# A graph kernel's gather units: from one feature group over four blocks in three banks to one block of rows with all 192 features in one bank, with norm factors and residuals on GpSimd

## The chip, the cores and the metric

The kernel runs on one core of a Trainium2 chip. The metric is the device time of one execution in microseconds (us). Before the change it was 928.25 us, the median of three runs (928.08 to 928.56 us).

Engines are named as the profile names them: PE is the matrix engine, PEld its loading of the stationary operand (the "weights"), DVE the vector engine, ACT the scalar engine, POOL GpSimd, SP the engine that issues the DMAs. Matmuls write to PSUM, which is used here in eight banks of 128 x 512 float32.

## The reference, cut to what matters

There are 128 graphs of 128 nodes with 64 features. Two layers follow each other, each with a residual and a layer norm:

```python
# layer 0
mask = adj > 0
h    = relu((x @ W1a)[:, :, None, :] + (x[:, :, None, :] - x[:, None, :, :]) @ W1b + b1)
hm   = einsum('bjkh,bjk->bjh', h, mask)             # 192 hidden features
x    = layernorm(x + hm @ W2 + deg[..., None] * b2)
# layer 1
agg  = einsum('bmn,bnd->bmd', adj, x)
h    = elu(elu(agg @ W1 + b1) @ W2 + b2)            # 128 hidden features
x    = layernorm(x + h @ W3 + b3)
```

Inside `relu` stands `a[j] + c[k]`, with a part that depends on node j alone and a part that depends on its neighbour k alone. Only neighbours count, and a row has few of them: about 6% of the entries of `adj` are positive.

## The kernel before, in words

Two graphs ("a pair") are worked on at a time, 64 pairs in all. In each pair the rows j of a graph are sorted by their number of neighbours. Each row then gets as many slots as its place in the sorted order allows, and slot s of row j holds its s-th neighbour. The table `BANKS` (line 43) gives four blocks of sorted rows with 9, 12, 22 and 15 slots a row: 504, 504, 176 and 330 slots, 1514 in all (the constant `E`). A second, dense path (`dense`, line 772) would take pairs that do not fit; it is not run in the profile.

**Gather units** (lines 704 to 744). A unit works in one of four PSUM banks (`edges`, `NE = 4`), and has three steps:

- *seed*: ACT copies the row part `aj` into the bank, repeated over the slots (L714);
- *gather*: PE adds the neighbour part `cp`, selected by the one-hot matrix `oh`, into the same bank. `cp` is held in three bfloat16 parts that add up to float32, so there are three matmuls, k = 0, 1, 2;
- *reduce*: DVE sums the absolute values over the slots into `sums` (L739).

A unit before is (pair, c, i). The feature group c = 0 or 1 means features 0 to 127 of the first or second graph; its matmuls (L725) use all 128 x 128 cells of the PE array. The group c = 2 holds features 128 to 191 of both graphs: for each k there are two matmuls (L729), each with 64 weight columns, one for the upper and one for the lower half of the partitions. The index i is one of three banks' worth of slots (504, 504, and 176 + 330 = 506). So a pair has 9 units with 3 matmuls (or 3 x 2 half-width ones) of some 504 columns each, and 12 seeds and 12 reduces, one for each block. The next unit on the same bank follows in the same lane (`lane`, line 755).

**The other steps of a pair.** `prepare`, `sort_x`, `project_a`, `sort_mask` and `turn` (lines 413 to 592) prepare a pair three rounds ahead: mask, degrees and ranks (L433 spreads the degrees over the partitions by matmul, L441 compares), the permutation (L450), the sorted x (L463, L465), the projections (L477 to L504), the correction for unused slots (L523 to L538), the slot numbers (L561) and the one-hot matrix `oh` (L572). `finish` (line 636) follows the units: correction (L642), product with W2 (L646 to L653), return to the given order with the residual added by a matmul with the identity (L662, L664), layer norm, layer 1 (L671 to L690), its last product with the residual again by a matmul with the identity (L694, L696), layer norm, and the output DMA (L700).

**The layer norm** (`norm`, line 594): ACT copies y out of PSUM (L597), DVE takes the statistics from PSUM (L603) and forms variance + eps (L605), POOL raises to the power -1/2 (L610), DVE forms the shift (L613), and two ACT activations apply scale and shift (L619).

**What sets the order.** `Flow` (line 278) is a planner that runs when the program is built. Every step is a `yield` with an engine, an estimated cost, the events it needs and the number of PSUM banks it takes out of four (`m0` to `m3`). The planner emits the steps, among those that could start next on an engine, by their due times; `ROUND` (13.0), `PACE` and `STEP` give these. Each engine then works its instructions in the emitted order, and semaphores hold what is not ready.

Of the kernel before, what the change touches and what calls it, by code (L numbers as in the profile page):

```python
# [39 lines left out]
EPS = 1e-5  # L40


BANKS = (((72, 128, 9),), ((30, 72, 12),), ((0, 8, 22), (8, 30, 15)))
# [3 lines left out]
def gnn_kernel(ctx: ExitStack, tc: tile.TileContext, x, adj, w1, b1, w2, b2,  # L47
# [12 lines left out]
    for blocks in BANKS:  # L60
        base, row = E, []
        for p0, p1, s in blocks:
            row.append((p0, p1, s, E - base))
            E += s * (p1 - p0)
        assert E - base <= 512
        LAY.append((base, E - base, row))
# [57 lines left out]
    nc.vector.memset(onesb, 1.0)  # L124
    small = const([P, P], BF16, "small")
    nc.vector.memset(small, 1.0 / P)
    mhalf = const([P, 2], F32, "mhalf")
    nc.vector.memset(mhalf, -0.5)
# [38 lines left out]
    for base, n, row in LAY:  # L167
        for p0, p1, s, off in row:
            nc.gpsimd.iota(slotf[:, base + off:base + off + s * (p1 - p0)],
                           pattern=[[2, s], [0, p1 - p0]], base=1, channel_multiplier=0,  # L170
                           allow_small_or_imprecise_dtypes=True)
    for p0, p1, s in sorted((b for bank in BANKS for b in bank), reverse=True):

        nc.vector.tensor_scalar(steps, jcol[:, 0:1], p1 / P, float(s - prev),
                                op0=OP.is_lt, op1=OP.mult)
        nc.vector.tensor_add(slots, slots, steps)
        prev = s
# [4 lines left out]
    for p0, p1, s in (b for bank in BANKS for b in bank):  # L182
        nc.vector.memset(srow[:, :, p0:p1], float(s))
# [52 lines left out]
    with tc.tile_pool(name="ps_s", bufs=2, space=bass.MemoryType.PSUM) as ps_s:  # L236
# [16 lines left out]
        nc.vector.tensor_sub(c3r, c3r, t[:, H1:H1 + O])  # L253
        nc.vector.tensor_scalar(v1s[F:F + 1], v1s[F:F + 1], 1.0, None, op0=OP.add)
# [95 lines left out]
def sparse(tc, env):  # L350
# [21 lines left out]
    ROUND = 13.0  # L372
    AHEAD = 3
    PACE = ROUND / (3 * NB)
# [23 lines left out]
    def dve(n):  # L398
        return 0.08 + n / 960
# [13 lines left out]
    def prepare(p):  # L413
# [21 lines left out]
        ev, key = yield ("PE", 2 * mm(N) + 0.1, [ev], 1, spread)  # L435
# [8 lines left out]
        ev, = yield ("DVE", 2 * dve(N) + 0.2, [ev], 0, rank)  # L444
        flow.give(key, ev)
        permb = d["permb"] = prep.tile([P, 2, N], BF16, name="permb")

        def permute():
            for s in range(2):
                nc.vector.tensor_scalar(permb[:, s, :], g.iotb, pos[:, s:s + 1], None,  # L450
                                        op0=OP.is_equal)
        ev, = yield ("DVE PORT", 0.36, [ev], 0, permute)
# [45 lines left out]
    def project_a(p, xT, ev):  # L498
# [30 lines left out]
        ev, eb = yield ("PE", 0.38, [have, event("mtp", p)], 1, short)  # L529
# [11 lines left out]
    def sort_mask(p, ev):  # L541
# [25 lines left out]
        for i, (base, n, row) in enumerate(LAY):  # L567
            for p0, p1, sl, off in row:
                w = p1 - p0
                c = slice(base + off, base + off + sl * w)  # L570
                e, = yield ("DVE PORT", 0.07 + sl * w / 860, [ev], 0,
                            lambda: nc.vector.tensor_tensor(  # L572
                                oh[:, :, c].rearrange("p b (s w) -> p b s w", w=w),
                                vp[:, :, p0:p1].rearrange("p b (o w) -> p b o w", o=1)
                                .to_broadcast([P, 2, sl, w]),
                                g.slotc[:, c].rearrange("p (b s w) -> p b s w", b=1, w=w)
                                .to_broadcast([P, 2, sl, w]),
                                op=OP.is_equal))
            happened(e, "oh", p, i)
# [14 lines left out]
    def norm(yps, ev, name):  # L594

        y = work.tile([P, 2, O], F32, name="y", bufs=6)
        evy, = yield ("ACT", act(2 * O), [ev], 0, lambda: nc.scalar.copy(flat(y), yps[:, :2 * O]))  # L597
        st = work.tile([P, 2, 3], F32, name="st", bufs=12)
        ve = work.tile([P, 2], F32, name="ve", bufs=12)

        def stats():

            nc.vector.bn_stats(st.rearrange("p s t -> p (s t)"),  # L603
                               yps[:, :2 * F].rearrange("p (s f) -> p f s", s=2))
            nc.vector.tensor_scalar(ve, st[:, :, 2], 1.0 / F, EPS, op0=OP.mult, op1=OP.add)  # L605
        ev, = yield ("DVE", 0.38, [ev, evy], 0, stats)
        flow.give(yps, ev)
        rs = work.tile([P, 2], F32, name="rs", bufs=12)
        ev, = yield ("POOL PORT", 0.72, [ev], 0,
                     lambda: nc.gpsimd.tensor_tensor(rs, ve, g.mhalf, op=OP.pow))  # L610
        nb = work.tile([P, 2], F32, name="nb", bufs=12)
        ev, = yield ("DVE", 0.1, [ev], 0,
                     lambda: nc.vector.scalar_tensor_tensor(nb, st[:, :, 1], -1.0, rs,  # L613
                                                            op0=OP.mult, op1=OP.mult))
        o = work.tile([P, 2, F], F32, name=name, bufs=6)

        def apply():
            for s in range(2):
                nc.scalar.activation(o[:, s, :], y[:, s, :], AF.Identity, bias=nb[:, s:s + 1],  # L619
                                     scale=rs[:, s:s + 1])  # L620
        ev, = yield ("ACT", 2 * act(F, 2), [ev], 0, apply)
        return o, ev
# [13 lines left out]
    def finish(p):  # L636
# [3 lines left out]
        ev, = yield ("POOL PORT", 1.05, [event("corr", p)] + [event("sums", p, c, i) for c in range(3)  # L640
                                                for i in range(NB)], 0,
# [19 lines left out]
        def unsort(t):  # L661
            nc.tensor.matmul(t[:, :2 * O], ident, flat(xx), start=True, stop=False)  # L662
            for s in range(2):
                nc.tensor.matmul(t[:, s * O:(s + 1) * O], d["permT"][:, s, :],  # L664
                                 ys[:, s * O:(s + 1) * O], start=False, stop=(s == 1))
        ev, t = yield ("PE", 0.6, [ev, event("permT", p)], 1, unsort)
        x1, ev = yield from norm(t, ev, "x1")

# [23 lines left out]
        def last(t):  # L692
            nc.tensor.matmul(t[:, :2 * O], onesb[:, :P], flat(g.c3p), start=True, stop=False)
            nc.tensor.matmul(t[:, :2 * O], ident, flat(x1), start=False, stop=False)  # L694
            for s in range(2):
                nc.tensor.matmul(t[:, s * O:(s + 1) * O], h2[:, s * N:(s + 1) * N], g.v3s,  # L696
                                 start=False, stop=(s == 1))
        ev, t = yield ("PE", 0.83, [ev], 1, last)
        o, ev = yield from norm(t, ev, "o")
# [3 lines left out]

    units = [(p, c, i) for p in range(NP) for c in range(3) for i in range(NB)]

    def unit(u, ev):
        p, c, i = units[u]
        d, e = S[p], edges[u % NE]
        base, n, blocks = LAY[i]

        def seed():
            for p0, p1, sl, off in blocks:
                w = p1 - p0
                nc.scalar.copy(e[:, off:off + sl * w].rearrange("p (s w) -> p s w", w=w),  # L714
                               d["aj"][:, c:c + 1, p0:p1].to_broadcast([P, sl, w]))
        ev, = yield ("ACT", 0.12 * len(blocks) + n / 1200,
                     [ev, event("aj", p), [T0[0] + pace(u)] if T0 else [0.0]], 0, seed)
# [3 lines left out]
        def gather():  # L721
            cp, oh = d["cp"], d["oh"]
            for k in range(3):
                if c < 2:
                    nc.tensor.matmul(e[:, :n], cp[:, k, c, 0:P], oh[:, c, base:base + n],  # L725
                                     start=False, stop=(k == 2), skip_group_check=True)
                else:
                    for s in range(2):
                        nc.tensor.matmul(e[s * HB:(s + 1) * HB, :n], cp[:, k, s, P:H],  # L729
                                         oh[:, s, base:base + n],  # L730
                                         start=False, stop=(k == 2), skip_group_check=True)
        ev, = yield ("PE", 3 * mm(n) + 0.06, [ev, event("cp", p), event("oh", p, i)], 0, gather)

        def reduce():
            if "sums" not in d:
                d["sums"] = work.tile([P, 3, N], F32, name="sums")
            for p0, p1, sl, off in blocks:
                w = p1 - p0
                nc.vector.tensor_reduce(d["sums"][:, c, p0:p1],  # L739
                                        e[:, off:off + sl * w].rearrange("p (s w) -> p w s", w=w),  # L740
                                        AX.X, OP.add, apply_absolute_value=True)
        ev, = yield ("DVE", 0.08 * len(blocks) + n / 960, [ev], 0, reduce)
        happened(ev, "sums", p, c, i)
# [233 lines left out]
```

## Time and profile before

| what | value |
|---|---|
| median of three runs | 928.25 us |
| the profiled execution: its time / its span in the trace | 928.32 us / 925.7 us |
| mean granted PE clock | 0.991 |
| busy share PE, PEld, DVE, ACT, POOL | 94%, 60%, 88%, 77%, 55% |
| matmul records | 6739 |
| the DMA engines' share (the main queue) | 8.1% |

The span is the time from the first to the last instruction of the profiled execution; 2.6 us of its own time lie outside. "Busy" is the union of an engine's instruction records. Those of PE overlap, since a matmul's record includes the time from its last column to its result. So the starts of matmuls tell how fast PE takes them, and the busy share does not. The profile gives, behind PE and PEld rows, the part of the array that an instruction uses as rows\*columns: 128\*128 is the whole array, 128\*64 one half of its columns, 64\*128 one half of its rows.

The first gather matmul starts at 42.2 us and the last one at 902.0 us of the span. What lies ahead is the set-up of constants and the preparation of the first pairs, and behind it the end of the last pair.

### The profile page before, as it was taken

How to read it: one execution, taken by the hardware profiler on the slowest of the kernel's cores; microseconds unless marked ns; L12 is line 12 of the kernel's file. 1: busy time of each engine (PE TensorE's matmuls, PEld its weight loads, DVE VectorE, ACT ScalarE, POOL GpSimd, SP SyncE). 2: the span in 40 equal slices, each digit the busy share in tenths (PEclk: the TensorE clock that was granted, in tenths of full speed). 3: DMA queues.
4: the chain of work that ended last, by engine and by line, in shares of the span. 5: the costliest groups of instructions: out<-in, count | busy, mean ns of one | idle time of the engine just before them, and what ended most of it. 6: DMA issues, size and time to landing. Idle time of an engine off the chain costs nothing. (4 is left out here: it accounts for less than half of the span.)

```text
span 925.7 us, 19643 instructions
## 1 busy us (share of the span) xinstructions
PE 867.1 (94%) x6739; PEld 556.4 (60%) x6740; DVE 813.8 (88%) x2278; ACT 717.3 (77%) x2050; POOL 506.6 (55%) x654
## 2 busy tenths in 40 slices
PE   2689999999999999999999999999999999999994
PEld 1456666665665665666665666666666666666663
DVE  7699889989989989989989989999999999999972
ACT  0577887788788788788788788888878887888772
POOL 1565555665556565556565556565556555555521
PEclk9999999999999999999999999999999999999996
DMA  1100100100110110110100010110011001000000
GB/s 29 43 10 21 25 15 21 24 21 16 24 24 13 24 24 14 24 25 12 25 23 15 22 24 12 25 24 16 21 25 24 16 21 25 16 23 22 7 8 12
DMA packets 63580, 18.84 MB, mean 20 GB/s; under 512 B 46257, under 2 KB 63474, under 8 KB 63474
## 3 DMA queue, kind: packets, MB, share of 16 engines
q1 hardware_dynamic: 63474, 17.52, 8.1%
q8 instruction: 55, 0.90, 0.4%
q14 instruction: 51, 0.42, 0.1%
HBM read 13.24 MB, written 4.19 MB: 19 GB/s over the span
## 5 line engine op out<-in xcount | busy, mean ns | idle before, releaser
L739 DVE TENSOR_REDUCE sums<-e 128x56 f32<-128x504 f32 (+3 forms) x768 | 395.0, 542 | 33.6 <-PE e L725 16.9
L714 ACT COPY e<-aj 128x504 f32<-128x504 f32 (+2 forms) x768 | 366.1, 486 | 74.3 <-DVE sums L739 67.4
L725 PE MATMUL e<-oh,cp 128*128 128x504 bf16 (+1 forms) x1152 | 281.7, 375 | 1.8 <-ACT e L714 1.7
L610 POOL TENSOR_TENSOR rs<-ve,mhalf 128x2 f32<-128x2 f32 x128 | 90.6, 708 | 228.2 <-DVE ve L605 223.9
L725 PEld LDWEIGHTS <-cp 128*128 128x128 bf16 x1152 | 106.1, 97 | 89.5 <-DVE sums L739 1.1
L729 PE MATMUL e<-oh,cp 128*64 128x504 bf16 (+1 forms) x1152 | 157.5, 382 | 1.1 <-ACT e L714 1.1
L572 DVE TENSOR_TENSOR oh<-vp,slotc 128x1008 bf16<-128x1008 bf16 (+2 forms) x256 | 153.9, 601 | 3.2 <-ACT vp L564 3.0
L642 POOL TENSOR_TENSOR hm<-sums,corr 128x384 f32<-128x384 f32 x64 | 73.6, 1151 | 45.8 <-DVE sums L739 42.3
L629 ACT ACTIVATE e<-m,mone 128x256 f32<-128x256 f32 x128 | 62.6, 489 | 32.4 <-PE m L688 30.9
L493 POOL CAST cp<-r 128x512 bf16<-128x512 f32 x64 | 48.9, 765 | 70.5 <-DVE r L490 70.4
L729 PEld LDWEIGHTS <-cp 128*64 128x64 bf16 x1152 | 53.9, 109 | 42.9 <-issue 18.2
L495 POOL TENSOR_TENSOR cp<-r,cp 128x512 bf16<-128x512 f32 x64 | 74.5, 1164 | 5.0
L518 POOL TENSOR_TENSOR sa<-aj,srow 128x384 f32<-128x384 f32 x64 | 64.4, 1007 | 21.2 <-ACT aj L511 21.1
L538 POOL TENSOR_TENSOR corr<-ea,sa 128x384 f32<-128x384 f32 x64 | 67.2, 1050 | 3.6 <-DVE ea L532 2.6
L419 POOL TENSOR_SCALAR mk<-adj 128x256 bf16<-128x256 f32 x64 | 54.8, 856 | 21.3 <-DMA xx<-in_x_dram 20.9
L632 DVE SCALAR_TENSOR_TENSOR h<-e,m 128x256 f32<-128x256 f32 x128 | 52.5, 410 | 10.1 <-ACT e L629 9.3
L490 DVE TENSOR_TENSOR r<-m,cp 128x256 f32<-128x256 f32 x128 | 53.1, 416 | 6.5 <-ACT cp L486 6.1
L597 ACT COPY y<-m 128x128 f32<-128x128 f32 x128 | 33.4, 261 | 28.7 <-PE m L664 22.0
L619 ACT ACTIVATE o<-y,nb,rs 128x64 f32<-128x64 f32 x128 | 51.2, 467 | 3.0 <-DVE nb L613 3.0
L486 ACT CAST cp<-m 128x256 bf16<-128x256 f32 x128 | 49.5, 388 | 3.2 <-PE m L479 3.2
L619 ACT ACTIVATE x<-y,nb,rs 128x64 f32<-128x64 f32 x128 | 49.3, 433 | 3.3 <-DVE nb L613 1.6
L651 PE MATMUL m<-w2h,hm 128*128 128x64 f32 x256 | 48.1, 289 | 0.0
(189 smaller groups left out, 1731.5 us busy)
## 6 DMA issues: line engine op xcount, KB each, us to landing
adj<-in_adj_dram SPq DMA_DIRECT2D x64, 128.0 KB, 2.3
xx<-in_x_dram SPq DMA_DIRECT2D x64, 64.0 KB, 2.2
out_dram<-o SPq DMA_DIRECT2D x64, 64.0 KB, 1.7
degs<-ys SPq DMA_DIRECT2D x64, 1.0 KB, 1.7
w1a<-in_L_gnn_W_dram SPq DMA_DIRECT2D x2, 48.0 KB, 2.2
w1b<-in_L_gnn_W_dram SPq DMA_DIRECT2D x2, 48.0 KB, 2.1
v1d<-in_L_gnn_W_dram SPq DMA_DIRECT2D x2, 32.0 KB, 2.1
v2s<-in_L_gnn_W_dram SPq DMA_DIRECT2D x1, 64.0 KB, 2.0
```

What stands on the lines that cost most here:

```text
L495: lambda: nc.gpsimd.tensor_sub(cp[:, 2], r1, cp[:, 1]))
L518: evs, = yield ("POOL PORT", 1.0, [have], 0, lambda: nc.gpsimd.tensor_mul(sa, aj, g.srow))
L538: ev, = yield ("POOL PORT", 1.05, [ev, evs], 0, lambda: nc.gpsimd.tensor_sub(corr, ea, sa))
L572: lambda: nc.vector.tensor_tensor(oh[:, :, c].rearrange("p b (s w) -> p b s w", w=w), vp[:, :, p0:p1].rearrange("p b (o w) -> p b o w", o= ...
L610: lambda: nc.gpsimd.tensor_tensor(rs, ve, g.mhalf, op=OP.pow))
L619: nc.scalar.activation(o[:, s, :], y[:, s, :], AF.Identity, bias=nb[:, s:s + 1], scale=rs[:, s:s + 1])
L629: lambda: nc.scalar.activation(e, z, AF.Exp, bias=g.mone))
L642: lambda: nc.gpsimd.tensor_sub(hm, d["sums"], d["corr"]))
L714: nc.scalar.copy(e[:, off:off + sl * w].rearrange("p (s w) -> p s w", w=w), d["aj"][:, c:c + 1, p0:p1].to_broadcast([P, sl, w]))
L725: nc.tensor.matmul(e[:, :n], cp[:, k, c, 0:P], oh[:, c, base:base + n], start=False, stop=(k == 2), skip_group_check=True)
L729: nc.tensor.matmul(e[s * HB:(s + 1) * HB, :n], cp[:, k, s, P:H], oh[:, s, base:base + n], start=False, stop=(k == 2), skip_group_check=True)
L739: nc.vector.tensor_reduce(d["sums"][:, c, p0:p1], e[:, off:off + sl * w].rearrange("p (s w) -> p w s", w=w), AX.X, OP.add, apply_absolute_ ...
```

## The change

- **Units.** `BLOCKS` takes the place of `BANKS`: nine blocks with 162, 66, 168, 112, 168, 154, 169, 154 and 170 slots (1323 in all). A unit is (pair, block). Its bank holds three parts side by side, each n slots wide: features 0 to 127 of the first graph, the same of the second, and features 128 to 191 of both. One seed, one reduce and one `oh` operation go with each block. For each k, PE runs two matmuls on the whole array and then two on half of its columns, and then goes to the next k.
- **Norm.** ACT copies y out of PSUM, POOL adds the residual, DVE takes the statistics from SBUF, and POOL forms variance + eps, the power and (for the first norm alone) the shift. The matmuls with the identity (L662, L694) are gone.
- **Last layer.** `v3s` and `c3r` have their mean over the outputs subtracted in the set-up, so that the last norm needs no shift.
- **Permutation.** The column numbers come through PSUM, by one more matmul beside those of the degrees, and the DVE compares from there; the bank is given back after it.
- `ROUND` is 11.8 and `PACE` is `ROUND / NB`; some cost estimates change.

```diff
-BANKS = (((72, 128, 9),), ((30, 72, 12),), ((0, 8, 22), (8, 30, 15)))
+BLOCKS = ((65, 83, 9), (0, 3, 22), (83, 104, 8), (3, 10, 16), (104, 128, 7), (10, 21, 14),
+          (21, 34, 13), (34, 48, 11), (48, 65, 10))
...
+        mean = temp([P, 2], F32, "mean")
+        for k, w in enumerate((v3s, c3r)):
+            nc.vector.tensor_reduce(mean[:, k:k + 1], w, AX.X, OP.add)
+            nc.vector.tensor_scalar(mean[:, k:k + 1], mean[:, k:k + 1], 1.0 / O, None, op0=OP.mult)
+            nc.vector.tensor_scalar(w, w, mean[:, k:k + 1], None, op0=OP.subtract)
...
-    ROUND = 13.0
+    ROUND = 11.8
...
+            nc.tensor.matmul(key[:, 2 * N:3 * N], g.small, g.iotb, start=True, stop=True)
...
-                nc.vector.tensor_scalar(permb[:, s, :], g.iotb, pos[:, s:s + 1], None,
+                nc.vector.tensor_scalar(permb[:, s, :], key[:, 2 * N:3 * N], pos[:, s:s + 1], None,
                                         op0=OP.is_equal)
...
-    def norm(yps, ev, name):
+    def norm(yps, ev, name, rest, shift):
...
+        ev, = yield ("POOL PORT", 0.45, [ev], 0, lambda: nc.gpsimd.tensor_add(y, y, rest))
...
+        def factors():
+            nc.gpsimd.tensor_scalar(ve, st[:, :, 2], 1.0 / F, EPS, op0=OP.mult, op1=OP.add)
+            nc.gpsimd.tensor_tensor(rs, ve, g.mhalf, op=OP.pow)
+            if shift:
+                for s in range(2):
+                    nc.gpsimd.tensor_scalar(nb[:, s:s + 1], st[:, s, 1:2], rs[:, s:s + 1], -1.0,
+                                            op0=OP.mult, op1=OP.mult)
...
-            nc.tensor.matmul(t[:, :2 * O], ident, flat(xx), start=True, stop=False)
...
-            nc.tensor.matmul(t[:, :2 * O], ident, flat(x1), start=False, stop=False)
...
-    units = [(p, c, i) for p in range(NP) for c in range(3) for i in range(NB)]
+    units = [(p, i) for p in range(NP) for i in range(NB)]
...
+        e = edges[u % NE][:, :3 * n]
...
             for k in range(3):
-                if c < 2:
-                    nc.tensor.matmul(e[:, :n], cp[:, k, c, 0:P], oh[:, c, base:base + n],
+                for s in range(2):
+                    nc.tensor.matmul(e[:, s * n:(s + 1) * n], cp[:, k, s, 0:P],
+                                     oh[:, s, base:base + n],
                                      start=False, stop=(k == 2), skip_group_check=True)
-                else:
-                    for s in range(2):
-                        nc.tensor.matmul(e[s * HB:(s + 1) * HB, :n], cp[:, k, s, P:H],
-                                         oh[:, s, base:base + n],
-                                         start=False, stop=(k == 2), skip_group_check=True)
+                for s in range(2):
+                    nc.tensor.matmul(e[s * HB:(s + 1) * HB, 2 * n:3 * n], cp[:, k, s, P:H],
+                                     oh[:, s, base:base + n],
+                                     start=False, stop=(k == 2), skip_group_check=True)
```

In the lists of instructions the gather has 36 matmuls a pair before and 108 after, and the whole of PE's list grows from 9594 to 18810 rows.

## The prediction

> **What bounds the kernel now.** I began with the page's busy shares, since they name the candidates, and then asked for stretches in the steady part.
>
> ```profile
> PE 867.1 (94%) x6739; PEld 556.4 (60%) x6740; DVE 813.8 (88%) x2278; ACT 717.3 (77%) x2050; POOL 506.6 (55%) x654
> 400.00:600.00 200.00, 195.48 (x1522) 124.47 (x1523) 182.49 (x498) 162.58 (x462) 114.88 (x144) 1.00 0.09 21
> ```
>
> The second line is one stretch, 400 to 600 us: PE, PEld, DVE, ACT and POOL busy, then the granted clock. PE is hardly ever without a record and DVE is next. But PE's records overlap, so I went to the starts of its matmuls. One round (a pair's worth of work) is the distance from one L523 matmul to the next: on average 13.64 us over the 45 rounds from the 11th to the 56th. Per round DVE is busy 182.49/200 x 13.64 = 12.45 us, ACT 11.1, POOL 7.8.
>
> In these 45 rounds (613.7 us) I called a start late if it came over 75 ns after the preceding matmul's columns had gone in (one column in 1/2.4 ns, twice that for float32), or over 170 ns where the part of the array changes. That waiting is 18.3 us, 0.41 us a round. So PE's own work is 13.24 us a round: it is the bound, with DVE 0.8 us behind. The gather has 273.4/45 = 6.08 us of it, the rest 7.16.
>
> Then the timeline of PE: start, length, line, array part, tile, count.
>
> ```profile
> 404.24 0.27 PE L547 MATMUL m<-permb,mk 128*128 128x128 bf16 x2
> 404.35 0.28 PE L550 MATMUL m<-identb,permb 128*128 128x128 bf16 x2
> 404.56 0.83 PE L729 MATMUL e<-oh,cp 128*64 128x504 bf16 x6
> 405.32 0.33 PE L463 MATMUL m<-ident,xx 128*128 128x128 f32 x1
> ...
> 406.78 0.83 PE L729 MATMUL e<-oh,cp 128*64 128x504 bf16 x6
> 407.44 0.38 PE L671 MATMUL m<-adjT,x 128*64 128x128 f32 x4
> 407.76 0.44 PE L587 MATMUL m<-ident,adj 128*128 128x128 f32 x2
> 408.12 0.83 PE L729 MATMUL e<-oh,cp 128*64 128x506 bf16 x6
> ```
>
> Four 128-column matmuls, each with new weights, start 55 ns apart (404.24, 404.35): short matmuls as such go at stream speed. After the fourth, L729 should start at 404.24 + 4 x 0.055 = 404.46; it starts at 404.56. L729 is three pairs of half-width matmuls, the two of a pair side by side (starts 4 ns apart in the trace). Its columns take 3 x 0.21, and the first pair 25 ns more, since its weights are loaded only then: done at 405.22. The next whole-array matmul starts at 405.32. So there is a gap of 0.10 us at each change of the array part. Where the part stays (L729 to L671, 406.78 + 0.66 = 407.44) there is none; from L671 to L587 and from L587 to L729 it is there again. Over 100 to 850 us I took all 413 such changes in the trace: none is under 94 ns, the medians by direction are 95 to 101. The queue of weight loads shows the same as idle time that no engine ended:
>
> ```profile
> PEld L547 <- issue: 26.6, 56, 0.7
> PEld L479 <- issue: 21.5, 64, 0.7
> PEld L729 <- issue: 18.2, 79, 0.6
> ```
>
> Each of these lines follows such a change in most rounds.
>
> **The gather after.** For each k the order is whole, whole, half, half: two changes for each k, six a unit, 54 a pair. From the two lists of PE instructions, over the same 45 rounds: 7.6 changes a round before, 57.0 after.
>
> Work for one k with n slots, from start to start: first whole matmul n/2.4 + 14 (after a change its successor starts 12 ns later than the usual 2, L547 behind L729), second n/2.4 + 95 (L550 to L729: 149 ns for 128 columns), the half pair 4 + n/2.4 + 25 + 96 (L729 to L547). Sum 1.25 n + 234 ns, a unit 3.75 n + 702. Over nine units with 1323 slots: 4.96 + 6.32 = **11.28 us**, where 6.08 stood. Fewer slots alone save 5.68 - 4.96 = 0.72 us of streaming; the changes cost 4.7 and the weights that are loaded late 0.9.
>
> A sentence of the Trainium skill is weighed here. "TensorEngine Tiling (Array Packing)", section "Key Properties", states that changing the tiling mode, not just the tile, drains the engine; it gives no price, so by it alone the sum has a sign and no size. "TensorE: Matmul & The Clock Gate", section "Back-to-back issue gap", gives about 81 ns a matmul at 128 columns and 131 at 512 in streams with weight loads. By that the gather would go from 36 x 131 = 4.7 us to about 108 x 83 = 9.0, also dearer by 4.3; but this trace has 55 and 213 ns, and the trace decides.
>
> **The rest of PE.** L662 goes (400.03 to 400.25 in the timeline, 0.22 us) and L694 (406.02 to 406.29, 0.28). The third matmul of the keys adds 0.055. So 7.16 - 0.50 + 0.06 = 6.72, and PE 11.28 + 6.72 = **18.0 us a round**.
>
> **DVE.** The reduces cost 332, 487 and 675 ns for 176, 330 and 504 elements: 150 + 1.04 per element. Twelve with 4542 elements become nine with 3969: 6.51 to 5.47. L605 (268 ns) and L613 (239) go, twice a round: -1.01. `oh` goes from 2.40 us (four operations) to nine operations on 2646 elements: 2.4 by the slope between 660 and 1008 elements (0.71 ns), 3.7 if the odd block widths cost the reduces' 1.04; I take 2.65, near the rows of the same operation. The comparison from PSUM (L450) lies between its 243 ns now and the 344 of L441, which reads the same bank: at most +0.2. DVE then has 10.6 us, at most 11.9: under 18.0, so none of it counts.
>
> **ACT.** Seeds: 591, 438 and 322 ns give 178 + 0.82 per element, 5.86 to 4.86. ACT 10.1: hidden.
>
> **POOL.** Adding the residual, 128 elements: between 203 ns (L428, 2 elements) and 1007 (L518, 384), 0.47 on the line. Variance and each shift are two-element work: 0.2 (L428) to 0.41 (L427). Twice (0.47 + 0.3) and two shifts of 0.2: +1.9, POOL 9.7, at most 10.5. Hidden too. The norm's chain gets some 1.4 us longer and its PSUM bank comes free earlier; the key bank is held some 0.4 us longer. A late aggregate (next L671) would hold all of PE behind it, units included. But a round that is 4 us longer gives each chain step more time than it has now; the waiting, 0.41 us now, I take as 0.1, with 0 and 1.0 as ends.
>
> **Set-up.** DVE has ten more two-column operations (0.19 apart, L174), five memsets (0.11) and six operations for the means (some 0.2): 3.7 us, of which its waits there (1.4 us for `c2r` alone) hide about half: +2. In the filling (46 to 100 us) PE idles 4 us by the stretches; being slower, it loses perhaps 3 of them. DMAs: the same transfers in the same order, 8% of the engines' time.
>
> **Sum.** 18.1 - 13.64 = 4.46 us a round, x 64 = 285 us; set-up +2, filling -3. The profiled execution took 928.32, the same as the median (928.25). 928 + 285 - 1 = **1212 us**, 30% slower.
>
> **The rivals.**
> - *The gap vanishes when matmuls are short*, because the next weights come in while the previous matmul runs. Then PE has 18.0 - 4.7 - 0.9 = 12.4 us a round, with DVE at 10.6 to 11.9. With today's waiting 12.8: 928 - 64 x 0.84 = **874 us**, faster. The point from which it decides: before is 13.64, so the 49.4 extra changes may cost 0.84/49.4 = 17 ns each, late weights included. Against it: L671 (107 ns of float32 columns) and L550 (53 ns) show the full gap. Chance 6%.
> - *Only one direction is paid*, since the half pair's loads go into a part already idle: 27 x 0.1 less, 18.1 - 2.6 = 15.5 us, 928 + 119 = **1047 us**. Against it: both directions show 94 ns and more. Chance 5%.
> - *PE pays and also waits, or its clock falls.* If the longer norm chain adds 1.5 us of waiting a round, **1305 us**. If the granted clock went to half because 30% of the time is gaps, streaming doubles (about +10 us a round, 1850 us). It stayed 1.00 in the filling, with PE busy 15.0 of 26 us, and fell only in the last 26 us (0.68). Chance 8%.
> - *The change doesn't do what it says*: the list after has 3456 whole and 3456 half gather matmuls in that order, so no chance is kept for it.
>
> **How the numbers follow.** The forecast keeps 81%. Its low end leaves out the late weights (-60 us) and takes 92 ns a gap: 1140. Its high end is waiting of 1.0 us a round: 1270. Faster by over 0.2% (about what a measurement of this kernel can tell from no change): 6%, from the first rival and what lies near it; the same: 1%; slower: 93%.
>
> **What would show it.** Gather matmuls starting 149 + (n - 128)/2.4 ns apart at a change; units 1.25 us long on PE; idle "issue" time ahead of the loads of L727 and L731; PE's busy share still high (its records cover the gaps), DVE near 60%, ACT near 56%. It is wrong if a half pair starts within 30 ns of the end of the whole matmul's columns, or if rounds are under 14 us.

## The result and the profile after

The changed kernel takes 1197.91 us (median of four runs, 1197.69 to 1198.70) against 928.40 us in the runs beside it: a ratio of 1.2905, with a 95% interval of 1.2882 to 1.2927. The forecast was 1212 us, 1140 to 1270. The profiled execution took 1197.69 us with a span of 1195.9 us and a mean granted clock of 0.994.

The page of the changed kernel: the engines' busy time, the chain of work that ended last, and the costly groups of the gather, each with busy time, mean length and the idle time ahead of it.

```profile
PE 1155.0 (97%) x11155; PEld 743.0 (62%) x11156; DVE 794.7 (66%) x2171; ACT 671.8 (56%) x1858; POOL 590.0 (49%) x1043
...
PE 95%; DVE 2%; SPq 1%; ACT 1%; issue 0%; POOL 0%; DMA 0%; DVEq 0%; ACTq 0%; POOLq 0%
...
L739 DVE TENSOR_REDUCE sums<-e 128x54 f32<-128x486 f32 (+8 forms) x576 | 353.7, 615 | 309.6 <-PE e L731 308.5
L727 PE MATMUL e<-oh,cp 128*128 128x162 bf16 (+6 forms) x3456 | 519.2, 232 | 0.7 <-DVE oh L575 0.5
L731 PE MATMUL e<-oh,cp 128*64 128x162 bf16 (+6 forms) x3456 | 441.3, 252 | 0.0
...
L731 PEld LDWEIGHTS <-cp 128*64 128x64 bf16 x3456 | 189.1, 106 | 210.4 <-issue 0.8
L727 PEld LDWEIGHTS <-cp 128*128 128x128 bf16 x3456 | 219.7, 98 | 115.4 <-issue 9.0
L575 DVE TENSOR_TENSOR oh<-vp,slotc 128x336 bf16<-128x336 bf16 (+6 forms) x576 | 221.0, 389 | 6.4 <-ACT vp L568 1.6
```

The reduces on the page of the kernel before:

```profile
L739 DVE TENSOR_REDUCE sums<-e 128x56 f32<-128x504 f32 (+3 forms) x768 | 395.0, 542 | 33.6 <-PE e L725 16.9
```

PE is now the only bound: 95% of the chain is PE, and the reduces, which waited 33.6 us for anything before, wait 309.6 us, nearly all of it for the last half-width matmul of their unit (L731). The matmul rows show no idle time at all (0.7 and 0.0 us), because each record runs on to its result and covers the gap behind it. The gaps stand in the rows of the weight loads: 210.4 us ahead of L731's and 115.4 us ahead of L727's.

The stretch from 400 to 600 us shows the same by engine (PE, PEld, DVE, ACT and POOL busy, granted clock):

```profile
400.00:600.00 200.00, 200.00 (x1960) 130.35 (x1960) 137.11 (x358) 118.25 (x327) 104.65 (x183) 1.00 0.07 16
```

PE has a record in flight all the time; DVE went from 182.49 of 200 us to 137.11. The clock is 1.00 as before, so the loss is not in the speed of a matmul. The timeline of PE shows where it is (start, length, line, array part, count):

```profile
600.02 0.31 PE L727 MATMUL e<-oh,cp 128*128 128x168 bf16 x2
600.26 0.26 PE L731 MATMUL e<-oh,cp 128*64 128x168 bf16 x2
600.46 0.32 PE L727 MATMUL e<-oh,cp 128*128 128x168 bf16 x2
600.71 0.26 PE L731 MATMUL e<-oh,cp 128*64 128x168 bf16 x2
600.91 0.32 PE L727 MATMUL e<-oh,cp 128*128 128x168 bf16 x2
601.16 0.27 PE L731 MATMUL e<-oh,cp 128*64 128x168 bf16 x2
601.35 0.27 PE L727 MATMUL e<-oh,cp 128*128 128x112 bf16 x2
```

Two whole-array matmuls of 168 columns are 0.14 us of streaming, but the half pair starts 0.24 to 0.25 us after the first of them; the pair is 0.07 us of streaming, but the next k starts 0.19 to 0.20 us behind it. One k takes 0.445 us, of which 0.21 are columns.

The accounts of the prediction, made again over the same 45 rounds of each trace (a round runs from one matmul of the correction to the next):

| us a round | before | forecast | after |
|---|---|---|---|
| gather on PE | 6.08 | 11.28 | 11.18 |
| PE's other work | 7.16 | 6.72 | 6.54 |
| waiting of PE | 0.41 | 0.1 | 0.09 |
| round | 13.64 | 18.1 | 17.81 |
| changes of the array part | 7.6 | 57.0 | 57.0 |

The difference of 4.17 us times 64 pairs is 267 of the 270 us.

### The profile page after: what moved, and what is told of

Its sections match the earlier page's. It is cut to its first block, busy times and chain, and to the rows that moved or that the text cites. A ratio compares the mean times of both kernels' runs of the same rounds, so it can differ in the third digit from the quotient of the medians.

```text
span 1195.9 us, 29198 instructions
## 1 busy us (share of the span) xinstructions
PE 1155.0 (97%) x11155; PEld 743.0 (62%) x11156; DVE 794.7 (66%) x2171; ACT 671.8 (56%) x1858; POOL 590.0 (49%) x1043
## 4 chain that ended last, share of the span: by engine, by line
PE 95%; DVE 2%; SPq 1%; ACT 1%; issue 0%; POOL 0%; DMA 0%; DVEq 0%; ACTq 0%; POOLq 0%
PE e L727 31%; PE e L731 27%; PE m L508 4%; PE m L481 3%; PE m L668 3%; PE m L656 3%; PE m L685 2%; PE m L699 2%; PE m L692 2%; PE m L469 2%; PE m L590 2%; PE m L651 1%; PE m L675 1%; PE m L467 1%; PE m L527 1%; PE m L551 1%
## 5 line engine op out<-in xcount | busy, mean ns | idle before, releaser
L739 DVE TENSOR_REDUCE sums<-e 128x54 f32<-128x486 f32 (+8 forms) x576 | 353.7, 615 | 309.6 <-PE e L731 308.5
L727 PE MATMUL e<-oh,cp 128*128 128x162 bf16 (+6 forms) x3456 | 519.2, 232 | 0.7 <-DVE oh L575 0.5
L731 PE MATMUL e<-oh,cp 128*64 128x162 bf16 (+6 forms) x3456 | 441.3, 252 | 0.0
L716 ACT COPY e<-aj 128x504 f32<-128x504 f32 (+6 forms) x576 | 312.9, 544 | 106.9 <-DVE sums L739 105.7
L731 PEld LDWEIGHTS <-cp 128*64 128x64 bf16 x3456 | 189.1, 106 | 210.4 <-issue 0.8
L727 PEld LDWEIGHTS <-cp 128*128 128x128 bf16 x3456 | 219.7, 98 | 115.4 <-issue 9.0
L575 DVE TENSOR_TENSOR oh<-vp,slotc 128x336 bf16<-128x336 bf16 (+6 forms) x576 | 221.0, 389 | 6.4 <-ACT vp L568 1.6
L603 POOL TENSOR_TENSOR y<-y,x 128x128 f32<-128x128 f32 x64 | 29.1, 455 | 186.2 <-ACT y L601 186.2
L559 ACT CAST mtp<-m 128x256 bf16<-128x256 f32 x64 | 23.9, 373 | 106.9 <-PE m L554 106.9
L499 POOL TENSOR_TENSOR cp<-r,cp 128x512 bf16<-128x512 f32 x64 | 74.0, 1156 | 0.5
L638 DVE SCALAR_TENSOR_TENSOR h<-e,m 128x256 f32<-128x256 f32 x128 | 53.0, 414 | 18.9 <-ACT e L635 18.1
L445 DVE SCALAR_TENSOR_TENSOR cmp<-m,keyc,tie 128x128 bf16<-128x128 f32 x128 | 39.9, 349 | 19.5 <-ACT y L601 11.9
```

The source lines that it names most:

```text
L499: lambda: nc.gpsimd.tensor_sub(cp[:, 2], r1, cp[:, 1]))
L575: lambda: nc.vector.tensor_tensor(oh[:, :, c].rearrange("p b (s w) -> p b s w", w=w), vp[:, :, p0:p1].rearrange("p b (o w) -> p b o w", o= ...
L716: lambda: nc.scalar.copy(e.rearrange("p (c s w) -> p c s w", c=3, w=w), d["aj"][:, :, p0:p1].rearrange("p c (o w) -> p c o w", o=1) .to_br ...
L727: nc.tensor.matmul(e[:, s * n:(s + 1) * n], cp[:, k, s, 0:P], oh[:, s, base:base + n], start=False, stop=(k == 2), skip_group_check=True)
L731: nc.tensor.matmul(e[s * HB:(s + 1) * HB, 2 * n:3 * n], cp[:, k, s, P:H], oh[:, s, base:base + n], start=False, stop=(k == 2), skip_group_ ...
L739: nc.vector.tensor_reduce(d["sums"][:, :, p0:p1], e.rearrange("p (c s w) -> p c w s", c=3, w=w), AX.X, OP.add, apply_absolute_value=True)
```

## The experiments

My theory: PE pays about 0.1 us at each change of the array part, and loads the first weights behind it late. The rivals: many short matmuls with a weight load each are dear as such; jumping between three places of one bank, or accumulating in them again, is what costs; part of the loss comes from the norm. All times below are medians, with 929 to 930 us for the kernel before on the same chip.

**The same instructions with fewer changes.** Each unit of the changed kernel issues its whole-array matmuls first.

```diff
-            for k in range(3):
-                for s in range(2): whole(k, s)
-                for s in range(2): half(k, s)
+            for part in (whole, half):
+                for k in range(3):
+                    for s in range(2):
+                        part(k, s)
```

(`whole` and `half` are names here for the two matmuls of the changed unit.)

> The changed kernel, but each unit issues its six whole-array matmuls first and then its three half-width pairs: same instructions, same columns, two changes of the array part a unit in place of six (21 a round in place of 57, by the list of instructions). Theory 'each change of the array part costs about 0.1 us, and the first weights after it are loaded late': per k the changed kernel takes 3 n/2.4 + 237 ns; here a whole unit takes 3.75 n + about 256 ns in place of 3.75 n + 711. That is 0.455 x 9 = 4.1 us a round less: round 13.7 us, 1198 - 64 x 4.1 = about 936 us (920 to 960). Rival 'many short matmuls are dear as such' (108 in place of 36): the order does not matter, 1198 us within 2%.

Measured: 947.8 us, ratio to before 1.019 (1.0173 to 1.0207). That is 250 us less with not one instruction fewer. A round is 13.83 us, of which the gather has 7.12, with 21.0 changes. PE's timeline, two units:

```profile
599.80 0.37 PE L727 MATMUL e<-oh,cp 128*128 128x162 bf16 x3
600.11 0.40 PE L732 MATMUL e<-oh,cp 128*64 128x162 bf16 x6
600.44 0.44 PE L590 MATMUL m<-ident,adj 128*128 128x128 f32 x2
...
602.97 0.35 PE L727 MATMUL e<-oh,cp 128*128 128x66 bf16 x6
603.25 0.28 PE L732 MATMUL e<-oh,cp 128*64 128x66 bf16 x6
```

Six whole-array matmuls of 66 columns are 0.165 us of streaming, and the half ones start 0.28 us behind the first. The first row counts three, since its list begins inside the unit. The three half pairs then start 52 and 36 ns apart, with 28 ns of columns each: no gap of 0.1 us stands between them. It came out 12 us above my sum. A round is 0.13 us longer than the 13.7 expected, and rounds near the beginning and the last twenty are longer (14.5 and 13.9 us); why stays open.

**Twice the changes.**

```diff
             for k in range(3):
-                for s in range(2): whole(k, s)
-                for s in range(2): half(k, s)
+                for s in range(2):
+                    whole(k, s)
+                    half(k, s)
```

> The changed kernel, but for each k the order is whole, half, whole, half: same instructions, twelve changes a unit (111 a round). Theory of the changes: per k 4 n/2.4 + 2 x (110 + 123) ns, since the halves no longer run side by side either, in place of 3 n/2.4 + 237: 290 ns x 27 = 7.8 us a round more, 1198 + 500 = about 1698 us (1650 to 1750). Rival 'number of matmuls': only the lost side-by-side running, 61 ns x 27 = 1.65 us a round, 1303 us.

Measured: 2396.4 us, ratio 2.581 (2.5732 to 2.5886). Both theories are far below. The page gives the reason: PE's busy share and, in 40 slices, the granted clock in tenths:

```profile
PE 2348.1 (98%) x11155; PEld 1341.8 (56%) x11156; DVE 798.2 (33%) x2171; ACT 676.4 (28%) x1858; POOL 586.2 (25%) x1043
...
PEclk9656566655555555555555555555556555555555
```

The clock was granted in full from 38.8 us, where its record begins, to 72.9 us of the span. Then it fell to half, and it went back and forth from there; the mean is 0.578. Three stretches:

```profile
42.00:60.00 18.00, 17.69 (x114) 10.52 (x114) 11.45 (x26) 6.41 (x18) 6.64 (x8) 1.00 0.01 1
80.00:100.00 20.00, 20.00 (x86) 9.79 (x85) 5.46 (x16) 5.08 (x14) 6.10 (x10) 0.50 0.00 1
1000.00:1100.00 100.00, 100.00 (x465) 57.65 (x464) 32.76 (x85) 29.05 (x81) 24.84 (x43) 0.53 0.04 9
```

While the clock was full, the price was what the theory says: between starts, whole to half mostly the columns plus 106 to 108 ns, half to whole the columns plus 122 to 124 ns (110 and 123 expected). At half clock (0.50) the columns take twice as long, and the rest rises only to about 110 and 141 ns. So the price of a change is confirmed at full clock, and the excess of the total over the sum goes with a second effect, the halved clock.

**Where the clock holds.** The order of the last experiment for k = 1 alone.

```diff
             for k in range(3):
-                for s in range(2): whole(k, s)
-                for s in range(2): half(k, s)
+                for part, s in (((whole, 0), (half, 0), (whole, 1), (half, 1)) if k == 1 else
+                                ((whole, 0), (whole, 1), (half, 0), (half, 1))):
+                    part(k, s)
```

> The changed kernel with the order whole, half, whole, half for k = 1 alone: 75 changes of the array part a round, between the changed kernel's 57 (granted clock 1.00 in the steady part) and the 111 of the kernel that alternates for every k (mean granted clock 0.578). Theory of the changes at full clock: 9 x 0.29 = 2.6 us a round more, 1198 + 167 = about 1365 us (1345 to 1390) with the granted clock near 0.99. Rival 'the clock falls as soon as there are more changes than the changed kernel has': clearly over 1400 us, up to about 1900, with the granted clock between 0.58 and 0.95.

Measured: 1361.6 us, ratio 1.466 (1.4635 to 1.468), granted clock 0.995; 20.37 us a round with a gather of 13.74. The 18 added changes, with the halves for k = 1 no longer side by side, cost 2.56 us a round, 2.6 expected. The clock holds at 75 changes a round (1.00 in the stretch from 400 to 600 us):

```profile
400.00:600.00 200.00, 200.00 (x1713) 129.08 (x1712) 119.96 (x312) 103.20 (x286) 90.70 (x158) 1.00 0.06 15
```

I worked out from each trace what share of the time columns stream into the array at full clock: 0.81 before, 0.56 after, 0.51 here (each over the 45 rounds), and 0.43 with 111 changes (48 to 70 us). So in these runs the clock stayed up at 0.51 and fell at 0.43. These are means over many units: single stretches of 3.4 us, the shortest time for which the clock fell in these traces, go down to 0.38 here without a fall. The share and the number of changes move together (75 and 111 a round), so the runs do not show which of them decides. The rule of the Trainium skill that bears on it ("TensorE: Matmul & The Clock Gate", section "What's actually happening"): the clock has two states, half and full, by how busy PE has been. In the trace with 111 changes the granted clock is 1.0 or 0.5 and nothing else, as it says. What share of work decides, it does not say, and these runs only bracket it.

**As many short matmuls, but no added changes.** The kernel before, each gather matmul cut in three.

```diff
-                    nc.tensor.matmul(e[:, :n], cp[:, k, c, 0:P], oh[:, c, base:base + n],
...
+                for a, b in ((0, 168), (168, 336), (336, n)):
...
+                        nc.tensor.matmul(e[:, a:b], cp[:, k, c, 0:P], oh[:, c, base + a:base + b],
```

(and the half-width ones likewise)

> The kernel before, with each gather matmul of some 504 columns cut in three of 168 with the weights loaded again each time: 108 gather matmuls a pair as in the changed kernel, but still 7.6 changes of the array part a round. Theory of the changes: 72 more matmuls at 2 to 3 ns each, 0.2 us a round, 928 + 12 = 940 us (928 to 955). Rival 'number of matmuls and weight loads': the whole growth of 4.2 us a round comes back, 58 ns for each added matmul, about 1195 us.

Measured: 935.6 us, ratio 1.0064 (1.0048 to 1.0081). The gather has 6.28 us in place of 6.08: 72 more matmuls, each with its weight load, cost 0.2 us a round, 2.8 ns each. In its timeline, nine whole-array matmuls of 168 columns:

```profile
400.72 0.82 PE L726 MATMUL e<-oh,cp 128*128 128x168 bf16 x9
401.37 0.42 PE L646 MATMUL m<-w2d,hm 128*128 128x128 f32 x2
```

The nine take 0.65 us, 72 ns each for 70 ns of columns. The rival of the matmul count is out.

**The same order and jumps, but the whole array throughout.**

```diff
-                    nc.tensor.matmul(e[s * HB:(s + 1) * HB, 2 * n:3 * n], cp[:, k, s, P:H],
+                    nc.tensor.matmul(e[:, 2 * n:3 * n], cp[:, k, s, 0:P],
```

> The changed kernel in its own order, but the two half-width matmuls of each k use whole-array weights (128 columns of cp in place of 64) and write all partitions of the same third of the bank. This leaves out the neighbour part of features 128 to 191 and puts other values there. Same number of matmuls, same jumps between the three parts of the bank, no change of the array part in the gather (5.1 a round are left). Theory of the changes: per k 4 n/2.4 + 10 ns, 6.9 us a round for the gather in place of 11.2, although more columns are streamed; round 13.5 us, about 926 us (910 to 950). Rival 'jumping between destinations in one bank, or accumulating there again, is what costs': 1198 us or, with the pairs no longer side by side, 1303 us.

Measured: 940.5 us, ratio 1.0111 (1.0094 to 1.0128): 257 us less than the changed kernel, though it streams a third more in the gather. Its timeline, the same place of a unit:

```profile
600.73 0.31 PE L727 MATMUL e<-oh,cp 128*128 128x168 bf16 x2
600.88 0.31 PE L731 MATMUL e<-oh,cp 128*128 128x168 bf16 x2
601.03 0.31 PE L727 MATMUL e<-oh,cp 128*128 128x168 bf16 x2
601.17 0.31 PE L731 MATMUL e<-oh,cp 128*128 128x168 bf16 x2
```

Two matmuls every 0.146 us (0.14 are columns), and no gap at the jumps. It is the array part and not the destination.

**The two halves of the change apart.** The units alone in the kernel before (its norm, identity matmuls and permutation kept), and everything but the units (with the old `BANKS`, units, `ROUND` and `PACE`).

The first is, against the kernel before:

```diff
-BANKS = (((72, 128, 9),), ((30, 72, 12),), ((0, 8, 22), (8, 30, 15)))
+BLOCKS = ((65, 83, 9), (0, 3, 22), (83, 104, 8), (3, 10, 16), (104, 128, 7), (10, 21, 14),
+          (21, 34, 13), (34, 48, 11), (48, 65, 10))
...
-    units = [(p, c, i) for p in range(NP) for c in range(3) for i in range(NB)]
+    units = [(p, i) for p in range(NP) for i in range(NB)]
```

and the second is the same edit the other way round, against the changed kernel.

> The kernel before with the new units alone (blocks, banks, oh operations, order of the gather, ROUND 11.8), its norm, identity matmuls and permutation kept. Theory: the changed kernel's 17.81 us a round + 0.50 - 0.06 for the matmuls that stay, DVE at 11.6 us hidden: 1198 + 28 = about 1226 us (1215 to 1240). Rival 'part of the loss comes from the norm and POOL': 1198 us or less.

Measured: 1225.95 us, ratio 1.3189 (1.3169 to 1.3209), as expected to the microsecond: the units carry all of the loss and more.

> The changed kernel with the units, banks, oh operations, ROUND and PACE of the kernel before: the change without its units (norm on POOL, no identity matmuls, centred last layer, column numbers through PSUM). Theory (the units carry the whole loss, the rest is a small gain on the bound, PE): PE 13.24 - 0.50 + 0.06 + 0.1 (one change of the array part more a round) = 12.9 us a round, with the waiting of before (0.41) 13.3; 928 - 64 x 0.34 = about 906 us (895 to 918). Rival 'the longer norm chain and POOL's added work hold PE up': 928 us or more.

Measured: 914.3 us, ratio 0.984 (0.9827 to 0.9854). The rest of the change is a gain of 1.6%, some 8 us less than my sum. The round is 13.36 us in place of 13.3: PE's other work fell by 0.31 us and not 0.34 (7.16 to 6.85), with 8.6 changes of the array part in place of 7.6. The 0.06 us a round make up about half of the 8 us; where the rest lies, outside these 45 rounds, stays open. Neither the norm's longer chain nor POOL's added work holds PE up: its waiting is 0.38 us.

**Fewer slots without the new units.** Could the 1323 slots' gain be had? I merged the new blocks to six in three banks, 1378 slots, on the kernel without the units, with `ROUND` at 13.0 and at 12.4, and ran the four blocks at 12.4 beside them.

```diff
-BANKS = (((72, 128, 9),), ((30, 72, 12),), ((0, 8, 22), (8, 30, 15)))
+BANKS = (((83, 128, 8), (3, 10, 16)), ((48, 83, 10), (34, 48, 11)), ((0, 3, 22), (10, 34, 14)))
```

> The change without its units, and the units of before with six blocks in three banks (472, 504 and 402 slots, 1378 in all, by merging the changed kernel's blocks): fewer slots with no change of the array part added. Theory: the gather streams 12 x 0.5 x 136 x 1.5/2.4 = 0.5 us less a round, PE 12.9 - 0.5 = 12.4; DVE 18 reduces in place of 12 (+0.9 - 0.4) 11.9, ACT 18 seeds (+1.1 - 0.3) 11.9; with waiting of 0.4 to 0.8 a round 12.8 to 13.2: 875 to 900 us. Rival 'now DVE and ACT are as full as PE and waits eat the gain': as the kernel without it, about 906 us.

> The six-block kernel with the planner's ROUND at 12.4 in place of 13.0, so that due times keep to the shorter round. Theory: steps are emitted in a slightly other order, 9.0 changes of the array part a round in place of 7.2 (+0.2 us), less waiting for late chains: within 1.5% of the six-block kernel, 870 to 905 us. Rival 'the planner's pace sets the round': 13.0 against 12.4 shows in full, 38 us less.

> The change without its units (four blocks, units of before) with the planner's ROUND at 12.4 in place of 13.0. Tells apart what the 911 us of the six-block kernel at 12.4 owe to. Theory 'ROUND only re-orders, the four-block kernel has PE work of 12.98 us a round and waiting of 0.38': 905 to 920 us, so fewer slots are worth little. Rival 'the shorter ROUND alone gives the gain the six blocks show against their own run at 13.0 (28 us)': about 886 us.

Measured, as ratios to before: six blocks at 13.0 938.7 us, 1.0097 (1.0081 to 1.0112); six blocks at 12.4 910.7 us, 0.9795 (0.9782 to 0.9809); four blocks at 12.4 903.1 us, 0.9717 (0.9704 to 0.973). My expectation for the first failed, and the others missed more narrowly: 910.7 us lies just above the 870 to 905 expected and 3.0% under the run at 13.0, where at most 1.5% was expected (its rival had 38 us, measured are 28), and 903.1 us lies just under 905 to 920. At 13.0 the gather did fall to 5.61 us, but PE's waiting rose to 1.21 us a round. Its longest waits (total us, times, longest):

```profile
PEld m L673 <- ACT ys L667: 47.3, 64, 1.1
...
PEld m L704 <- DVE h L642: 40.3, 57, 1.5
PE m L704 <- DVE h L642: 30.9, 52, 0.9
```

L673 returns the rows to their order, L704 is the last product; in nearly every round they come to their turn before ACT and DVE have their input, and hold up everything behind them on PE. So the rival named there was right that waits eat the gain, and they ate more than it said (938.7 us where it had 906). At 12.4 the four blocks finish 8 us earlier than the six, but not everywhere: from the 11th to the 40th round the six blocks take 12.85 us a round against 13.37, and in the last twenty 14.09 against 12.86. So the gain of fewer slots is there, and is lost in the late rounds; why these are long stays open. The value of `ROUND` alone is worth 28 us with six blocks and 11 with four; how the order makes them I did not take apart. The fastest version is the change without its units at `ROUND` 12.4: 903.1 us, 2.8% under the kernel before. The kernel before was not run at 12.4, so how much of the step from 1.6% to 2.8% it would gain by itself is not known.

## Why the prediction was right, step by step

- **What bounds.** PE, not DVE: right. It follows from the starts; the busy shares alone (PE 94%, then 97%) would have shown nothing of the 270 us.
- **The price of a change of the array part.** Right. In the trace after, between 100 and 1100 us, whole to half costs 94 ns at least and 97 in the median (1571 changes); the trace before had 94 and 101. Half to whole is 98 at least and 123 in the median, the 98 and the 25 ns of late half-width weights that the sum had as two terms. Three experiments that alter only the order or the array part confirm it (order: 250 us less and, with 18 changes more, 2.56 us a round; array part: 257 us less), and the rivals of the matmul count and of the destination are out. That the page "TensorEngine Tiling (Array Packing)" has the engine drained at a change of mode agrees in sign.
- **The late weights.** Right: behind a change, the second whole-array matmul starts 12 to 13 ns after the columns of the first, where 2 to 3 are usual (the sum had 14), and the half pair takes 25 ns extra.
- **PE's other work.** Forecast 6.72, measured 6.54, the largest miss of the sum, 0.18 us or 12 us in all. The units alone bring it from 7.16 to 6.96. The sum kept all changes that steps outside the gather had paid for, and added the 54 of the units; by the traces the former went from 5.3 to 4.0 a round, 0.13 us. The rest stays open.
- **The waiting** (0.1 forecast, 0.09 measured): right.
- **DVE, ACT and POOL hidden.** Right in effect. DVE's size was off: 137.11/200 x 17.81 = 12.2 us a round, where I had 10.6 and at most 11.9. The reduces' busy time fell by 0.64 us only (395.0 to 353.7 over 64 pairs), because their records overlapped and I had summed lengths. `oh` came to 221.0/64 = 3.45 us where I took 2.65: nine operations cost more than four, in a way that the last section shows. ACT 10.5 (forecast 10.1), POOL 9.3 (9.7).
- **Set-up and filling.** The first gather matmul starts at 42.5 us, where it started at 42.2: the +2 us did not come.
- **The rivals.** The gap did not vanish for short matmuls, nor did it fall on one direction only. The clock did not fall in the changed kernel before its last 14 us, but the fear was near: with twice the changes it did. One argument against that rival was a misreading: the 1.00 of the stretch from 20 to 46 us is no sign that the clock stays up with PE half idle, for the record of the clock begins only at 35.4 us in that trace, and ahead of it the two matmuls of L547 (128 columns) start 0.107 us apart (32.61 and 32.72 us), which is half clock, against 0.055 from 38.56 us on.
- **The rows that would show it.** The idle time of the weight loads came, but the profile names its cause in only 9.8 us of it ("issue"); the rest stands without a releaser.

## What to carry to other kernels

Before reordering matmuls, list them with the array part that each uses and count the neighbours that differ: here each cost 0.1 us, more than the columns of one matmul, and grouping the same matmuls by part took 250 us off 1198. Read the price from the starts of matmuls; a busy share near 100% hides the gaps, and even a halved clock.
A change made of several parts is worth taking apart: here the part that looked large lost 32% by itself, and the small ones gained 1.6%, or 2.8% with the planner's pace set anew.

## What the runs showed of the hardware

Gaps can cost twice. At a streaming share of 0.51 the granted clock stayed full, and at 0.43 it fell to half, which took the kernel with 111 changes from the 1698 us of the sum to 2396.

An `oh` operation on DVE can be held up by POOL. The smallest `oh` operation of the changed kernel (132 elements) took 235 to 247 ns in the 29 cases in which no POOL operation overlapped it, and 896 to 1232 ns in the 32 cases in which POOL's subtraction of L499 (1156 ns) did; in each of the 32, it ended 107 to 113 ns after L499. No run takes L499 away, so the cause is inferred from these times. Undisturbed, the `oh` operations take 243 ns for 132 elements, 327 for 308 and 339 for 340, so their fixed part is near 180 ns, and an odd block width costs little (351 ns for 13 rows, 328 for 24, with 338 and 336 elements). It hardly touched the path here: a gather matmul waited for an `oh` operation once, for 0.5 us.
